# Spreading the last element's rounds by what a tick loads, another PSUM bank for the gate's 1x1, and result rows stored from GpSimd

## The chip, the cores and the metric

The kernel runs on one core of one Trainium2 chip. The metric is the device time of one execution in microseconds (us); lower is better. The core has a matrix engine (TensorE, "PE" in the profile, with its weight loads shown apart as "PEld"), VectorE ("DVE"), ScalarE ("ACT"), GpSimd ("POOL") and SyncE ("SP"), which here only issues DMAs. Each engine carries out its own instructions strictly in the order in which they were written.

## The reference, cut to what matters

The input x is 8 elements of 8 channels of 512x512, in float32. Two layers are each added to their input:

```python
x = x + L0(group_norm(x))        # a few Fourier modes: "spectral" work
x = x + L1(group_norm(x))
# L1(x), per element:
grid = x
for _ in range(15):              # a coupled map lattice
    mapped = 3.9 * grid * (1 - grid)
    grid = 0.85 * (0.7 * mapped + 0.3 * conv3x3_per_channel(mapped)) + 0.15 * x
cml = clip(grid, 1e-4, 1 - 1e-4)
nca = sigmoid(conv1x1(relu(conv3x3(x, 8 -> 128)), 128 -> 8))
g   = sigmoid(conv1x1(relu(conv3x3(concat[x, cml, nca], 24 -> 8)), 8 -> 8))
return g * cml + (1 - g) * nca
```

## The kernel before, in words

Everything is in float32. There are three kinds of work per element, and one schedule that mixes them.

**Steps.** The 15 map steps run on slabs (class `Slabs`): four slabs for the first four channels (`halves[0]`), then four slabs and one `Tail` slab, which holds the last rows, for the other four. One step of one slab is `convolve` (line 524: 48 matrix products into a pair of PSUM tiles) and `settle` (line 537: VectorE adds, line 543: ScalarE squares), and then `renew` exchanges edge rows between slabs by two to four small DMAs from the GpSimd queue (lines 570 and 571); the tail slab gets its edge row through DRAM by SP (lines 580, 641, 646). Step 13 also has a long GpSimd operation on the slab (line 547). A slab's inputs `dE` and `dO` are loaded by SP (line 495), scaled by GpSimd (line 516) and squared once by ScalarE (line 502). A step of a slab needs the slab's own previous step, four or five steps earlier in the order.

**Rounds.** `Hidden.round` is the wide 3x3 convolution (line 723), four image rows in each round, 128 rounds per element; its two halves are evacuated by ScalarE (line 729) and VectorE (line 731). After every second round `Hidden.point` forms the 1x1 channel sum (line 742) in bank 0 of a PSUM tile. It is copied into the tile `y` (line 749) or added to it (line 751); after every fourth round a sigmoid (line 755) finishes `y`, and `y` (128 x 512, 256 KB) is stored to the DRAM plane `nca` (line 758). There is one buffer for `y`, so line 749 of the next four rounds waits until the store has been read out.

**Gates.** `Gate` makes 12 finished image rows; 43 gates make an element. `load` has six DMAs on SP (lines 778 and 783), `conv` is the gate's 3x3 (line 793) with operations on GpSimd (798) and VectorE (799, 803), `point` is its 1x1 (line 810), a sigmoid (814) and a product on GpSimd (816), `finish` adds on VectorE (821) and stores to the output from SP (828). The gates of an element run one element late, beside the steps of the next one. The gates of the last element have no steps to run beside.

**The order.** It is written out by a planner in Python and kept as it is (`keep_order`). A tick (`turn`, `work`) is: two steps, into the PSUM tile pairs `near` and `far`; then loads (`transfers`); then 0, 1 or 2 rounds, into the same pairs; then, where they are due, the gate's 3x3 (bank 0 of `near[0]`), the channel sum (bank 0 of `near[1]`) and the 1x1 of the gate before (bank 1 of `near[0]`). After a tick of two rounds the pairs change places for the next tick; after a tick of one round `near` and `far` change places only for the rest of that tick. Small things put off with `later(1, ...)`, the store of `y` among them, are issued at the end of the tick.

An element has 67 or 68 ticks. In elements 0 to 6 all 128 rounds lie in them, mostly two to a tick. In the last one `ROUNDS_LAST` = 48 rounds are spread evenly over 67 ticks, so a tick has one or none; the 43 gates of element 6 run in the same ticks as early as they can, up to two loaded ahead (`limit` 2). Around the change of phase, from `AHEAD` = 12 steps before the end of the first half to 6 after it, `Phase.fetch` loads the five slabs of the second half; this is called the load window below (ticks 24 to 33 of the element). Only three tile slots are then left to the gates.

After the last step comes the tail of the program: 46 ticks without steps, which hold the remaining 80 rounds, two to a tick, and the 43 gates of the last element, with `limit` 3; its last gate ticks have no round.

Of the kernel before, what the change touches and what calls it, by code (L numbers as in the profile page):

```python
# [43 lines left out]
N = 512  # L44
# [6 lines left out]
FLOOR = -1.0e14  # L51
RT = 32
GR = 12
ROUNDS, ROUNDS_LAST, FIRST_ROUNDS = 128, 48, 8
LONG, LATER, NEXT = -1, -2, -3
GATES_FROM, SPECTRAL_FROM = 1, 2

# [8 lines left out]
SLOTS, SHARED, MORE, LEAST = 20, 5, 8, 3  # L66
AHEAD, PAUSE = 12, 6
# [44 lines left out]
def view(t, offset, dims):  # L112

    return bass.AP(tensor=t.tensor, offset=t.offset + offset, ap=[list(d) for d in dims])
# [3 lines left out]
def conv_layers(ctx: ExitStack, tc: tile.TileContext, a, out):  # L118
    nc = tc.nc
# [9 lines left out]
    class Slots:  # L129
# [4 lines left out]
        def __init__(self, most):  # L134
            self.most, self.held = most, {}
# [15 lines left out]
    sets, shared = Slots(SLOTS), Slots(SHARED)  # L151
# [7 lines left out]
    pairs = [pp.tile([P, 2, N], F32, name=f"pair{i}") for i in range(4)]  # L159
# [4 lines left out]
    def later(ticks, work):  # L164
        put_off.append((now[0] + ticks, work))

    def tick(end=False):
        now[0] += 1
        due = [w for at, w in put_off if end or at <= now[0]]
        put_off[:] = [] if end else [(at, w) for at, w in put_off if at > now[0]]  # L170
        for work in due:
            work()
# [483 lines left out]
    class Phase:  # L656
# [23 lines left out]
        def squares(self, n):  # L680
            while self.squared < len(self.sets) and sets.room():
                if not self.ready(self.squared, 0, n + 2):
                    break
                self.sets[self.squared].square()
                self.squared += 1
# [9 lines left out]
    class Hidden:  # L695
# [42 lines left out]
        def point(self, ps):  # L738

            for r, h in self.hs:  # L740
                for g in range(4):
                    nc.tensor.matmul(  # L742
                        ps[32 * g : 32 * g + 32], w_u[:, r % 4], h[:, g],
                        start=(r == self.hs[0][0]), stop=(r == self.hs[-1][0]),
                        tile_position=(0, 32 * g),
                    )
            if self.hs[0][0] % 4 == 0:
                self.y = wk.tile([P, N], F32, tag="y", name="y", bufs=1)
                nc.scalar.copy(self.y, ps)  # L749
            else:  # L750
                nc.vector.tensor_tensor(self.y, self.y, ps, ALU.add)  # L751
            self.hs.clear()
            if r % 4 == 3:
                y, r0 = self.y, 4 * (r - 3)
                nc.scalar.activation(y, y, AF.Sigmoid, bias=b_u)  # L755

                def store():
                    nc.sync.dma_start(
                        out=view(self.e.nca, (1 + r0) * C * N, [[N, P], [1, N]]), in_=y
                    )  # L760
                    self.e.rows = r0 + 16

                later(1, store)
# [129 lines left out]
    class Others:  # L893


        def __init__(self):
            self.before, self.after, self.limit = None, None, 2
            self.mapped, self.paused = deque(), False
            self.loaded, self.convolved, self.pointed = deque(), deque(), deque()
            self.longs = 0  # L900

        def feed(self, t):
            if self.mapped and not (self.before and self.busy()):
                self.before = self.mapped.popleft()
            e, after = self.before, self.after
            spectral = after and after.pieces
            spectral = spectral and (t >= SPECTRAL_FROM or not e)
            kept = max(0, after.most() - len(after.x)) if spectral else 0
            while e and e.gates and t >= GATES_FROM and not self.paused:
                if len(self.loaded) == self.limit or shared.room() - kept < 2:  # L910
                    break
                if e.rows < min(e.gates[0].r0 + GR + 1, N) or len(e.mapped) <= 2 * SETS:
                    break
                g = e.gates.popleft()
                g.load()
                self.loaded.append(g)
            if spectral:
                after.fetch()
# [62 lines left out]
    def element(b):  # L981
        e = Element(b)
        phase(e.halves[0])
        phase(e.halves[1] + [e.tail])
        elements.append(e)
        return e

    e = element(0)
# [3 lines left out]
    others = Others()  # L992
    for n in count():
# [8 lines left out]
        first = phases[0]  # L1002
# [10 lines left out]
    def work(steps, rounds, e, after, transfers, squares=lambda: None):  # L1013

        settled = iter(())
        near, far = pairs[:2], pairs[2:]
        for (s, step), ps in zip(steps, (near, far)):
            s.convolve(step, ps)
            next(settled, None)
            settled = s.settle(step, ps)  # L1020
            next(settled)
            others.finish()
        others.finish()
        transfers()
        for ps in (near, far)[:rounds]:
            e.hidden.round(ps, after, settled)
        next(settled, None)
        squares()

        if rounds == 2:  # L1030
            pairs.reverse()
        elif rounds:
            near, far = far, near
        point = rounds and e.hidden.n % 2 == 0
        gate = others.gate(near[0][:, 0])
        others.spectral((far[0], far[1]) if gate else (near[0], far[0] if point else near[1]))
        if point:
            e.hidden.point(near[1][:, 0])
        if not others.point(near[0][:, 1]):
            others.spectral([near[0] if gate or point else near[1]])  # L1040
        tick()
        squares()

    def turn(at, rounds, e, after, t):


        now_phases = [p for p in phases if at < p.end + 2]

        def transfers():
            others.feed(t)  # L1050
            for p in now_phases:
                p.fetch(at)

        def squares():
            for p in now_phases:
                p.squares(at)

        for p in now_phases:
            p.prepare(at)
        steps = [slots[i] for i in (at, at + 1) if 0 <= i < len(slots)]  # L1060
        work(steps, rounds, e, after and after.hidden, transfers, squares)
# [3 lines left out]
    at = 0  # L1065
    for b in range(B):
        e = elements[b]
        after = element(b + 1) if b + 1 < B else None
        others.after = after
        done, rounds = e.hidden.n, ROUNDS if after else ROUNDS_LAST  # L1070
        first, second = phases[2 * b : 2 * b + 2]
        ticks = (second.end - at + 1) // 2
        for t in range(ticks):
            assert not after or t < ticks - 5 or not after.pieces
            others.paused = ticks - t <= PAUSE
            if others.paused or first.end - AHEAD <= at < first.end + 6:
                shared.most = LEAST
            else:
                shared.most = MORE if first.at + 6 <= at < first.end else SHARED
            sets.most = SLOTS - shared.most  # L1080
            more = done + (t + 1) * (rounds - done) // ticks - e.hidden.n
            turn(at, min(more, 2 - e.hidden.n % 2), e, after, t)
            at += 2
        assert e.hidden.n == rounds
        assert not others.mapped
        others.mapped.append(e)


    others.after, others.limit, others.paused, shared.most = None, 3, False, SLOTS
    while e.hidden.n < ROUNDS or others.mapped or others.busy():  # L1090
        turn(at, min(2, ROUNDS - e.hidden.n), e, None, GATES_FROM)
        at += 2
    tick(end=True)
    keep_order(tc)
# [54 lines left out]
```

## Time and profile before

| | |
|---|---|
| three runs | 9471.27, 9478.95 and 9484.94 us; median 9478.95 |
| profiled execution | 9485.99 us, of which the span is 9484.2 us |
| busy: PE, DVE, ACT, POOL | 9052.0, 5647.2, 4078.4, 3362.1 us |
| steps on PE (line 524) | 3696.7 us |
| rounds on PE (line 723) | 2854.9 us |
| channel sums, gate 3x3, gate 1x1 on PE (lines 742, 793, 810) | 1062.7, 963.8, 370.3 us |
| store of `y` from SP (line 758) | 256 of them, 256 KB each |
| DMA traffic | 1327 MB, mean 140 GB/s |

A row of a timeline reads: start in us, duration in us, engine and source line, operation, output<-inputs, count; in brackets the time that the engine had been idle before it, and what ended the wait. A row of stretches reads: the stretch, its length, the busy time of each engine with the number of instructions, the clock granted to PE as a share of full speed, the busy share of the DMA engines, GB/s. A row of waits reads: who waited for whom, us in total, how often, the longest.

### The profile page before, as it was taken

What the parts mean: (1) busy time and instruction counts of PE and PEld (TensorE: products, weight loads), DVE (VectorE), ACT (ScalarE), POOL (GpSimd) and SP (SyncE); (2) the same over time, 40 slices, a digit from 0 to 9 for tenths busy, and PEclk for the clock granted to TensorE, in tenths of its full rate; (3) what the DMA queues carried; (4) which work ended last, traced back from release to release, by engine and by line L of the source; (5) the groups of instructions that cost most, each with busy time, mean ns of one, the idle gap of its engine ahead of it and who ended that gap; (6) DMA issues with size and microseconds to landing.
All of it is one profiled execution on the core that took longest, in us unless ns stands there. A gap on an engine that the chain in (4) does not pass through costs nothing. (4 is left out here: it accounts for less than half of the span.)

```text
span 9484.2 us, 331791 instructions
## 1 busy us (share of the span) xinstructions
PE 9052.0 (95%) x148976; PEld 4062.8 (43%) x148976; DVE 5647.2 (60%) x5820; ACT 4078.4 (43%) x4285; POOL 3362.1 (35%) x4422
## 2 busy tenths in 40 slices
PE   6999999999999999999999999999999999988998
PEld 3444444444444444444444444444444444333433
DVE  5665566655665556655566555665566655545555
ACT  2444444444444444444444444444444444434432
POOL 3232334334333343433434343243433433444322
PEclk9999999999999999999999999999999999999999
DMA  4241365555655655655655556565575665675287
GB/s 151 83 128 37 95 170 138 144 138 141 154 151 140 142 132 147 166 132 133 158 134 161 144 118 169 126 162 141 117 181 134 162 138 125 144 164 132 65 207 192
DMA packets 698558, 1327.07 MB, mean 140 GB/s; under 512 B 146938, under 2 KB 152442, under 8 KB 669650
## 3 DMA queue, kind: packets, MB, share of 16 engines
q1 hardware_dynamic: 594432, 1249.10, 52.1%
q0 software_dynamic: 100352, 55.61, 2.9%
q8 instruction: 1171, 19.19, 0.9%
q14 instruction: 249, 2.04, 0.1%
q10 hardware_dynamic: 2354, 1.14, 0.0%
HBM read 977.48 MB, written 270.61 MB: 132 GB/s over the span
## 5 line engine op out<-in xcount | busy, mean ns | idle before, releaser
L524 PE MATMUL pair<-m,band 32*32 32x512 f32 x103680 | 3696.7, 603 | 164.2 <-issue 105.7
L543 ACT ACTIVATE m<-m 128x1024 f32<-128x1024 f32 x2016 | 2128.5, 1056 | 2425.9 <-DVE m L537 2358.8
L723 PE MATMUL pair<-cols,w_p 32*128 32x511 f32 (+1 forms) x24576 | 2854.9, 603 | 59.8 <-DVE m L537 16.4
L524 PEld LDWEIGHTS pair<-m,band 32*32 32x32 f32 x103680 | 1999.4, 103 | 1793.0 <-issue 1006.5
L570 POOL DMA_DIRECT2D m<-m x1568 | 864.1, 551 | 3929.1 <-ACT m L543 3853.4
L537 DVE SCALAR_TENSOR_TENSOR m<-pair,dO 128x1024 f32<-128x1024 f32 x1152 | 1356.6, 1220 | 1187.3 <-PE pair L524 1023.6
L723 PEld LDWEIGHTS pair<-cols,w_p 32*128 32x128 f32 x24576 | 1302.0, 186 | 1627.7 <-issue 1147.9
L537 DVE SCALAR_TENSOR_TENSOR m<-pair,dE 128x1024 f32<-128x1024 f32 x1008 | 1187.8, 1220 | 1106.6 <-PE pair L524 912.8
L731 DVE TENSOR_SCALAR h<-pair,b_p 128x1024 f32<-128x1024 f32 x1024 | 1313.3, 1283 | 870.2 <-PE pair L723 865.3
L729 ACT ACTIVATE h<-pair,b_p 128x1024 f32<-128x1024 f32 x1024 | 1141.4, 1115 | 894.4 <-PE pair L723 893.7
L742 PE MATMUL pair<-h,w_u 128*32 128x512 f32 x8192 | 1062.7, 611 | 42.4 <-ACT h L729 40.8
L793 PE MATMUL pair<-gin,w_g 128*32 128x511 f32 (+1 forms) x8256 | 963.8, 600 | 3.7 <-DMA gin<-nca 2.9
L816 POOL TENSOR_TENSOR mix<-mix 96x512 f32<-96x512 f32 x344 | 438.3, 1274 | 1336.2 <-ACT mix L814 1267.7
L571 POOL DMA_DIRECT2D m<-m x1568 | 844.9, 539 | 30.0 <-issue 25.9
L742 PEld LDWEIGHTS pair<-h,w_u 128*32 128x32 f32 x8192 | 245.2, 110 | 699.8 <-issue 347.3
L755 ACT ACTIVATE y<-y,b_u 128x512 f32<-128x512 f32 x256 | 185.1, 723 | 821.8 <-DVE y L751 821.8
L793 PEld LDWEIGHTS pair<-gin,w_g 128*32 128x32 f32 x8256 | 234.8, 110 | 683.0 <-issue 458.1
L798 POOL TENSOR_TENSOR mix<-mix 96x512 f32<-96x512 f32 x344 | 443.8, 1290 | 73.2 <-DMA mix<-nca 69.1
L547 POOL TENSOR_SCALAR dO<-dO 128x2048 f32<-128x2048 f32 x72 | 391.9, 5443 | 112.4 <-DVE m L537 111.4
L749 ACT COPY y<-pair 128x512 f32<-128x512 f32 x256 | 150.2, 587 | 637.8 <-PE pair L742 510.2
L516 POOL TENSOR_SCALAR dO<-dO,base 128x512 f32<-128x512 f32 x288 | 207.1, 730 | 580.8 <-DMA dO<-xn 502.6
L810 PE MATMUL pair<-mix,w_g 128*32 128x512 f32 x2064 | 370.3, 605 | 42.7 <-DVE mix L803 39.6
(89 smaller groups left out, 3280.9 us busy)
## 6 DMA issues: line engine op xcount, KB each, us to landing
gin<-xn SPq DMA_DIRECT2D x344, 384.0 KB
cols<-xn SPq DMA_DIRECT2D x256, 512.0 KB
x<-in_x SPq DMA_DIRECT2D x120, 1024.0 KB
gin<-cml SPq DMA_DIRECT2D x344, 320.0 KB
gin<-nca SPq DMA_DIRECT2D x344, 320.0 KB
dE<-xn SPq DMA_DIRECT2D x288, 256.0 KB
dO<-xn SPq DMA_DIRECT2D x288, 256.0 KB
mix<-xn SPq DMA_DIRECT2D x344, 192.0 KB
```

Source lines behind the costliest of these rows:

```text
L524: nc.tensor.matmul(ps[h // 2][32 * t : 32 * t + 32, h % 2], band[at, self.channel(step - 1, h, t), dx], m[at, t, dx : dx + N], start=(n == ...
L537: nc.vector.scalar_tensor_tensor(u[:, at], ps[q], FLOOR, d[:, at], ALU.max, ALU.add)
L543: nc.scalar.square(u[:, at], u[:, at])
L570: nc.gpsimd.dma_start(out=view(tb, rb, dims), in_=view(ta, ra, dims))
L571: nc.gpsimd.dma_start(out=view(ta, ra + s, dims), in_=view(tb, rb + s, dims))
L723: nc.tensor.matmul(ps[g // 2][:, g % 2, lo:hi], w_p[p, dx, i % 2], self.cols[p, i // 2, at : at + hi - lo], start=(n == 0), stop=(n == 2), ...
L729: nc.scalar.activation(h[:, :2], ps[0], AF.Relu, bias=b_p)
L731: nc.vector.tensor_scalar(h[:, 2:], ps[1], b_p, 0.0, ALU.add, ALU.max)
L742: nc.tensor.matmul(ps[32 * g : 32 * g + 32], w_u[:, r % 4], h[:, g], start=(r == self.hs[0][0]), stop=(r == self.hs[-1][0]), tile_position ...
L793: nc.tensor.matmul(ps[32 * j : 32 * j + 32, lo:hi], gband[:, dx], gin[:, j, at : at + hi - lo], start=(n == 0), stop=(n == 2), tile_positi ...
L798: nc.gpsimd.tensor_tensor(d, d, ng, ALU.subtract)
L816: nc.gpsimd.tensor_tensor(d, d, mix[: GR * C, 2], ALU.mult)
```

## The change

Five things are changed. The store of `y` is issued by GpSimd instead of SP. The gate's 1x1 goes to bank 1 of `near[1]` where the tick has no channel sum, and stays in `near[0]` where it has one. The pairs also change places after a tick without a round but with a gate's 3x3, and, in the last element alone, after a tick of one round and nothing else. The last element gets 56 rounds instead of 48 in its ticks: two in each tick of the load window, the others spread over the rest; and no gate is loaded in every fifth tick (`closed`). In the tail the other 72 rounds are spread over 39 ticks rather than put two to a tick from the start, and up to four gates are loaded ahead instead of three.

By the written order this gives, in the last element's ticks, 12 more rounds and 6 more channel sums in the load window (19 and 10 instead of 7 and 4, with 5 gate convolutions in both), and 4 rounds and 2 channel sums fewer outside it (37 and 18 instead of 41 and 20, with 38 gate convolutions in both). The tail has 46 ticks as before: 33 full ones (two rounds, channel sum, gate), four with one round and a gate, and five with a gate alone, where it had 38 full ones and four with a gate alone. In elements 1 to 6 two gate 1x1s each change their bank.

```diff
-ROUNDS, ROUNDS_LAST, FIRST_ROUNDS = 128, 48, 8
+ROUNDS, ROUNDS_LAST, FIRST_ROUNDS = 128, 56, 8
...
                 def store():
-                    nc.sync.dma_start(
+                    nc.gpsimd.dma_start(
                         out=view(self.e.nca, (1 + r0) * C * N, [[N, P], [1, N]]), in_=y
                     )
...
-            while e and e.gates and t >= GATES_FROM and not self.paused:
+            while e and e.gates and t >= GATES_FROM and not (self.paused or self.closed):
...
-        if not others.point(near[0][:, 1]):
+        last = others.point((near[0] if point else near[1])[:, 1])
+        if not last:
             others.spectral([near[0] if gate or point else near[1]])
+        if rounds == 0 and gate or rounds == 1 and not (gate or point or last or after):
+            pairs.reverse()
...
+        quota = [(t + 1) * (rounds - done) // ticks for t in range(ticks)]
+        if not after:
+            loads = [first.end - AHEAD <= at + 2 * t < first.end + 6 for t in range(ticks)]
+            left = rounds - done - 2 * sum(loads)
+            quota = [
+                2 * sum(loads[: t + 1]) + (t + 1 - sum(loads[: t + 1])) * left // (ticks - sum(loads))
+                for t in range(ticks)
+            ]
...
-            more = done + (t + 1) * (rounds - done) // ticks - e.hidden.n
+            more = done + quota[t] - e.hidden.n
+            others.closed = not after and t % 5 == 4
...
-    others.after, others.limit, others.paused, shared.most = None, 3, False, SLOTS
-    while e.hidden.n < ROUNDS or others.mapped or others.busy():
-        turn(at, min(2, ROUNDS - e.hidden.n), e, None, GATES_FROM)
+    others.after, others.limit, others.paused, others.closed = None, 4, False, False
+    shared.most = SLOTS
+    done, ticks = e.hidden.n, -(-N // GR) - 4
+    for t in count():
+        if e.hidden.n == ROUNDS and not others.mapped and not others.busy():
+            break
+        more = min(ROUNDS, done + (t + 1) * (ROUNDS - done) // ticks) - e.hidden.n
+        turn(at, min(more, 2 - e.hidden.n % 2), e, None, GATES_FROM)
         at += 2
```

More of the change, by code (lines that the diff above doesn't have):

```diff
@@ L897, in __init__ @@
             self.before, self.after, self.limit = None, None, 2
-            self.mapped, self.paused = deque(), False
+            self.mapped, self.paused, self.closed = deque(), False, False
             self.loaded, self.convolved, self.pointed = deque(), deque(), deque()
```

## The prediction

> **What bounds the kernel now.** I read the page first, then stretches, then who PE waited for in the last element, then the timeline where it waits longest.
>
> ```profile
> PE 9052.0 (95%) x148976; PEld 4062.8 (43%) x148976; DVE 5647.2 (60%) x5820; ACT 4078.4 (43%) x4285; POOL 3362.1 (35%) x4422
> PE   6999999999999999999999999999999999988998
> ```
>
> PE is the bound: nine tenths or more in nearly every slice. The exceptions are the first slice, which the change leaves alone, and the last seven. So time can only come from work taken off PE, and the change takes none off, or from PE's idle time, which is 432 us in all. The stretches say where that lies (last element's ticks: 8073 to 8998, its load window 8412 to 8586; then the tail).
>
> ```profile
> 0.00:8073.00 8073.00, 7780.64 (x129534) 3545.01 (x129537) 4915.12 (x5125) 3569.16 (x3747) 2858.98 (x3820) 0.99 0.55 138
> 8073.00:8412.00 339.00, 311.79 (x5814) 131.54 (x5798) 181.32 (x181) 137.91 (x142) 150.10 (x211) 0.98 0.63 145
> 8412.00:8586.00 174.00, 135.85 (x2356) 54.41 (x2340) 76.71 (x70) 56.79 (x59) 87.78 (x102) 0.89 0.71 164
> 8586.00:8998.00 412.00, 376.17 (x7488) 173.71 (x7460) 228.75 (x216) 171.38 (x173) 156.98 (x205) 0.99 0.39 93
> 8998.00:9060.00 62.00, 47.39 (x372) 18.07 (x367) 18.36 (x19) 13.39 (x16) 7.33 (x6) 0.83 0.71 179
> 9060.00:9437.00 377.00, 377.00 (x3340) 134.83 (x3335) 212.30 (x196) 125.06 (x142) 87.79 (x71) 1.00 0.86 209
> 9437.00:9484.20 47.20, 23.20 (x152) 5.18 (x144) 14.64 (x16) 4.72 (x7) 13.15 (x10) 0.79 0.51 126
> ```
>
> In the last element's 925 us PE is idle for 27.2 + 38.2 + 35.8 = 101 us, and in the load window its clock also falls to 0.89. In the tail it is idle 14.6 us at the start and 24.0 us at the end, and never in the 377 us between. What it waited for from 8073 to 8998:
>
> ```profile
> PE pair L810 <- DVE mix L803: 27.1, 25, 4.5
> PE pair L742 <- ACT h L729: 17.6, 10, 6.8
> PE pair L524 <- ACT mix L814: 13.6, 13, 3.1
> PE pair L524 <- ACT h L729: 9.0, 8, 1.3
> ```
>
> The first, third and fourth are small waits in almost every tick, one of each kind here:
>
> ```profile
> 8815.19 1.06 PE L810 MATMUL pair<-mix,w_g 128*32 128x512 f32 x6 [1.08 <-DVE mix L803]
> 8817.17 5.40 PE L524 MATMUL pair<-m,band 32*32 32x512 f32 x156 [0.92 <-ACT mix L814]
> ...
> 8840.42 6.17 PE L524 MATMUL pair<-m,band 32*32 32x512 f32 x173 [1.26 <-ACT h L729]
> ```
>
> The 1x1 waits until VectorE has read the gate's 3x3 out of the same tile. The next step waits until ScalarE has read the 1x1, or the only round, out of the pair that the step wants. In full ticks of two rounds the same pieces lie far enough apart. The second wait, 17.6 us, is the load window: ScalarE stands at a slab's square until `dE` has landed (43.8 us in this element), and a round's evacuation queues behind it. At the start of the tail it is SP:
>
> ```profile
> 9002.98 7.31 SPq L758 DMA_DIRECT2D nca<-y  x1
> 9019.18 0.59 ACT L749 COPY y<-pair 128x512 f32<-128x512 f32 x1 [15.04 <-DMA nca<-y]
> 9019.82 5.09 PE L723 MATMUL pair<-cols,w_p 32*128 32x512 f32 x24 [11.56 <-ACT y L749]
> ```
>
> The store of `y` stood 7.31 us in SP's issue behind 21 stores of `cml` (its median is 0.34 us), the one `y` buffer stayed taken, and PE stood for 11.56 us.
>
> **Part 1, the bank and the exchange of pairs.** Nothing is added on PE. Outside the load window the last element has 11 ticks without a round but with gate and 1x1 (each loses about 1.08 + 0.92 = 2.0 us), 13 of one round, gate and 1x1 (0.87 us each, one row of that wait) and 6 of one round alone (1.26 us). All have other PE work of one tick in between afterwards: 22.0 + 11.3 + 7.6 = 41 us. After the change five ticks have a 1x1 and neither round nor gate; there the pairs do not change and the step waits 0.9 us for the sigmoid: 4.5 us back. Net 36 us. The work just after a wait also runs slower: a tick of one round, sum, gate and 1x1 holds 15.6 us of PE work after such a tick against 14.6 us elsewhere. With some seven of these I take 8 us. In elements 1 to 6 a 0.87 us wait goes once each, and the other exchanged 1x1 already waited for nothing: 5 us.
>
> **Part 2, rounds into the load window.** Its ten ticks gain 12 rounds of 2.85 us and 6 sums of 2.0 us, 46 us of PE work. What ten ticks with two rounds cost under the same loads is seen one element earlier. The first row is element 6's window, 20 rounds and 10 sums; the second is the last element's, 7 rounds and 4 sums:
>
> ```profile
> 7341.00:7504.70 163.70, 158.24 (x2673) 75.80 (x2671) 115.73 (x118) 79.98 (x82) 79.18 (x88) 0.99 0.66 178
> 8412.50:8585.70 173.20, 135.05 (x2326) 53.82 (x2321) 76.41 (x70) 56.79 (x59) 87.28 (x102) 0.89 0.71 163
> ```
>
> So the time there is set by the loads, and work put into it is nearly free. PE work after: ten pairs of steps at 6.28 us (a tick with nothing else), 19 rounds, 10 sums, five gates at 2.78 + 1.06 us: 62.8 + 54.2 + 20 + 19.2 = 156 us. With idle time between element 6's 5.5 us and element 5's 12 us, and a little for the clock, 167 us: 6 us less than now. Outside the window 4 rounds and 2 sums go and one 1x1 comes: 14 us less.
>
> **Part 3, the tail.** Its gates now come every 10.63 us (36 of them), then 7.38, 7.31, 7.24 and 9.08 us where there is no round; the first two distances are 9.78 and 16.97. Sum from first to last: 440.5 us. After: 33 at 10.63 (350.8), two at 7.8 (less one round), two that PE could do in 5.8 but that I hold at the 7.3 us of the ticks without rounds, which wait for loads, and five without rounds at 6.4 (between PE's 3.9 and 7.3, since a gate more is loaded ahead): 413 us. Add 4 us for a wait at the start, which stays. The first gate comes 30 us after 8998 now. Its loads are queued behind the same `cml` stores, so it comes at 28 us even with the store of `y` elsewhere; the two single-round ticks leave less work to cover it, and that work is done later in the count above. 16 us follow the last gate in both. Tail: 461 instead of 486 us, 25 less. DMA moves about 92 MB there; at 209 GB/s and a 0.86 share the engines' full rate is estimated at 243 GB/s, hence a floor of 380 us.
>
> **Part 4, the store from GpSimd.** 256 issues leave SP, where SP stood 868 us for the sigmoid over elements 0 to 6; but behind the store SP next meets line 828, which waits 2244 us for line 821, so little is freed. The nearest row for an issue on GpSimd is line 570: 552 ns median for 24 KB or 8 KB, 32 packets each. This store has at least 128 rows, so 0.55 to 4 x 0.55 = 2.2 us; I take 1.1. It is placed at the end of a tick, ahead of the next edge exchange on GpSimd, which idles there for 7.76 us before line 570 at 8815. If that cover is gone, as at step 13 where operations of 5.4 us follow one another, 16 such places cost up to 16 x 2.2 = 35 us. From below: the 124.9 us that squares wait for `dE` might fall by a tenth, -12 us. I take -3, since most ticks lie near the idle row.
>
> The Trainium skill, "DMA: Bandwidth & Descriptors", section "Issuing engines are not separate DMA queues", speaks against this part: whichever engine issues, the transfers share the same DMA engines, so only issue time is saved. The 7.31 us above is issue time, but the landing at 9019 came later than that. By the rule the two waits of 11.56 and 2.79 us at the tail's start stay, and the sum would be some 10 us less gain; no sum here needs it.
>
> **Sum.** Window -6, outside it -36 - 8 - 14 = -58, tail -25, elements 1 to 6 -5, store -3: -97 us. Against the profiled execution, 9485.99 us, that is 9389; its median of three is 7 us lower, so 9382, rounded to 9385 us.
>
> **Rivals.** *Only part comes* (0.20): more rounds in the window bring more evacuations behind a late `dE`, the 38 us idle stays there and the tail's DMAs do not get ahead. Window 156 + 38 = 194 instead of 167 (+27), tail's single-round and last ticks at 10.6 (+20): 9432, or 9420 to 9450. For it: loads cannot be seen to come earlier. Against: element 6's window. *More comes* (0.08): SP, free of the store, gets edge rows and slabs in earlier in all elements, and half of their 30 us idle each goes for two or three: 9345. *No change* (0.05): PE's waits reappear at the next hand-over of a bank, 9460 to 9498. *Slower* (0.07): the store holds GpSimd before the edge exchange in every element. At 1.1 us each, all exposed, 256 x 1.1 = 282: 9667. It decides from 95 / 256 = 0.37 us exposed per store. Against it: GpSimd is busy 35%, and the next exchange must await a step and its squares first.
>
> **How the numbers follow.** The forecast, 9385, has 0.60 (9350 to 9420). The range leaves out the slower case, no change, the upper edge of the partial one and some of the larger gain: 9342 to 9448. About 0.2%, 19 us, can be told from no change: faster 0.88 (0.60 + 0.20 + 0.08), same 0.05, slower 0.07.
>
> **What would show it.** Right: in the last element waits of 1x1 for line 803 and of steps for line 814 nearly gone; ten window ticks of about 167 us with two rounds each; line 749 not waiting for its store at the tail's start; gates of the tail still 10.63 us apart in full ticks. Wrong: GpSimd's line 758 at over 2 us with line 570 late behind it, the window at 190 us or more, or a longer wait for the first gate's loads than 30 us.

## The result and the profile after

The changed kernel takes 9507.52 us (median of 17 runs, 9477.40 to 9526.49), the kernel before 9482.33 us (17 runs, 9463.76 to 9503.76). The ratio is 1.0026, 95% interval 1.0015 to 1.0036: slower by about 25 us, where 97 us less were forecast. The profiled execution of the changed kernel took 9518.56 us with a span of 9516.7, against 9485.99 and 9484.2 before, so the two traces differ by 32.5 us.

The page of the changed kernel, its busy line and TensorE's line of slices:

```profile
PE 9080.2 (95%) x148976; PEld 4064.1 (43%) x148976; DVE 5655.6 (59%) x5820; ACT 4072.7 (43%) x4285; POOL 3505.6 (37%) x4678
PE   6999999999999999999999999999999999999989
```

Of the three slices below nine tenths among the last five one is left, and the kernel is still slower. PE ran as many matrix products as before, in 28 us more. The stretches of the changed kernel, cut at the same places of the program (elements 0 to 6; the last element before, in and after its load window; start, middle and end of the tail):

```profile
0.00:8149.00 8149.00, 7817.80 (x129534) 3543.38 (x129536) 4904.18 (x5125) 3565.02 (x3747) 2976.90 (x4040) 0.99 0.54 137
8149.00:8462.00 313.00, 293.14 (x5643) 125.99 (x5634) 169.99 (x167) 132.19 (x135) 144.28 (x210) 0.96 0.55 129
8462.00:8649.00 187.00, 169.99 (x2695) 73.43 (x2678) 100.81 (x85) 73.44 (x76) 90.83 (x106) 0.94 0.68 160
8649.00:9049.00 400.00, 378.43 (x7432) 172.88 (x7431) 229.24 (x219) 170.03 (x174) 172.87 (x219) 0.97 0.48 113
9049.00:9110.00 61.00, 37.34 (x372) 13.87 (x352) 21.12 (x19) 9.91 (x11) 6.70 (x6) 0.80 0.74 175
9110.00:9470.00 360.00, 360.00 (x3182) 128.10 (x3178) 211.79 (x190) 116.71 (x135) 96.30 (x86) 1.00 0.88 219
9470.00:9516.70 46.70, 23.49 (x185) 6.45 (x174) 18.44 (x19) 5.39 (x8) 17.75 (x13) 0.86 0.59 142
```

The first row has it: the last element, in whose ticks and tail nearly all of the change but the store lies, starts 76 us later. There the same 129,534 products were 37 us longer busy (7780.6 before) and PE stood some 39 us longer. The last element and the tail gained 43.5 us. By ticks, each taken from the start of VectorE's first addition of a step to the next tick's (a profiled execution is one run, and runs of one kernel lie up to 50 us apart, so what a part is worth is taken from medians below):

| us, profiled executions | before | after | difference | forecast |
|---|---|---|---|---|
| elements 0 to 6 | 8073.5 | 8149.5 | +76.0 | -8 |
| last element, load window | 173.1 | 187.0 | +13.9 | -6 |
| last element, other ticks | 741.6 | 712.5 | -29.1 | -58 |
| tail | 496.0 | 467.7 | -28.3 | -25 |

In the last element the prediction's list of waits before the change leaves out two rows that stand above its last one:

```profile
PE pair L524 <- issue: 17.5, 12, 3.1
PE pair L524 <- DMA m<-m: 9.8, 4, 4.0
```

The waits of the changed kernel there (who waited for whom, us in total, times, longest):

```profile
PE pair L524 <- DMA m<-m: 17.1, 7, 3.8
PE pair L524 <- issue: 11.1, 7, 3.6
PE pair L524 <- ACT mix L814: 10.7, 5, 2.2
PE pair L742 <- ACT h L729: 6.8, 7, 5.3
```

Of the 27.1 us for line 803 2.0 are left, and of the 9.0 us of steps for line 729 0.8. Line 814 is down to the five ticks with a 1x1 and neither round nor 3x3, at 2.1 us each instead of the 0.9 that I took. At the top are now steps that wait for the edge exchange (`m<-m`), 17.1 us where it was 9.8, and steps whose wait shows no cause in the profile ("issue"). At the start of the tail:

```profile
9064.38 8.32 SPq L778 DMA_DIRECT2D gin<-xn  x1
...
9087.05 4.53 PE L793 MATMUL pair<-gin,w_g 128*32 128x512 f32 x24 [23.28 <-DMA gin<-nca]
```

The store of `y` no longer stands behind the stores of `cml`; the gate's first load stands there in its place for 8.32 us, and PE waits 23.28 us for the gate.

### The profile page after: what moved, and what is told of

Same layout as the page of the kernel before. It is cut to its first block, busy times and chain, and to the rows that moved or that the text cites. A ratio compares the mean times of both kernels' runs of the same rounds, so it can differ in the third digit from the quotient of the medians.

```text
span 9516.7 us, 331665 instructions
## 1 busy us (share of the span) xinstructions
PE 9080.2 (95%) x148976; PEld 4064.1 (43%) x148976; DVE 5655.6 (59%) x5820; ACT 4072.7 (43%) x4285; POOL 3505.6 (37%) x4678
## 5 line engine op out<-in xcount | busy, mean ns | idle before, releaser
L723 PE MATMUL pair<-cols,w_p 32*128 32x511 f32 (+1 forms) x24576 | 2867.6, 605 | 44.6 <-DVE m L537 20.9
L821 DVE SCALAR_TENSOR_TENSOR mix<-mix,back 96x512 f32<-96x512 f32 x344 | 334.9, 974 | 143.9 <-POOL mix L816 143.9
L803 DVE TENSOR_SCALAR mix<-pair,b_g 128x512 f32<-128x512 f32 x344 | 257.7, 749 | 201.5 <-PE pair L793 200.3
```

Of the source, the lines that this page charges most:

```text
L723: nc.tensor.matmul(ps[g // 2][:, g % 2, lo:hi], w_p[p, dx, i % 2], self.cols[p, i // 2, at : at + hi - lo], start=(n == 0), stop=(n == 2), ...
```

## The experiments

Each of the twelve was timed beside the kernel before on the same chip, in three batches on three chips (first to fourth, fifth to eighth, ninth to twelfth), so runs of different batches are compared by their ratios. "First" to "twelfth" below follows the order of the runs.

### Which part costs: first and second

The first is the kernel before with only the store of `y` moved; the second is all of the change but that.

```diff
 # first, on the kernel before
-                    nc.sync.dma_start(
+                    nc.gpsimd.dma_start(
 # second, on the changed kernel
-                    nc.gpsimd.dma_start(
+                    nc.sync.dma_start(
```

> The kernel before, with the store of y issued by GpSimd and nothing else of the change. In the changed kernel's profiled execution the last element began 76.0 us later than before (8149.5 against 8073.5 us), and everything from there on was 43.5 us shorter. Theory A, the store does it by its place in GpSimd's order (it stands for the sigmoid, and slab scaling and edge exchange stand behind it): elements 0 to 6 longer by 50 to 75 us here too, 9530 to 9555 us. Theory B, the store does it by its path (256 KB through GpSimd's DMA queue, shared with the edge exchange): the same number. Theory C, SP is let go earlier and its loads collide with the edge exchange: the same number. Theory D, it is not the store: no change within 10 us of 9482.

> The changed kernel, with the store of y issued by SP as before. Theories A, B and C: elements 0 to 6 as before, the last element and the tail keep most of their gain of 43.5 us: 9435 to 9450 us. At the tail's start the wait for the store of y may come back, which takes some 5 us of it. Theory D: like the changed kernel, about 9507.

Measured: the store alone 9545.71 us, ratio 1.0068 (1.0052 to 1.0085); the rest alone 9442.81 us, ratio 0.996 (0.9947 to 0.9974). The product is 1.0028, within the interval of the change's own 1.0026. So one word of the diff costs some 66 us (against 9479.15 there), and the other parts gain some 36.

### What of the store costs: third, fourth, fifth, tenth, twelfth

Four theories stood: the store's place in GpSimd's order (A); its path through GpSimd's queue (B); SP, let go by it, issues its own loads too early (C); something other than the store (D, gone with the first run).

The third puts the store, in elements 0 to 6, behind the next tick's first edge exchange on GpSimd; the fourth issues it from ScalarE, which computes the sigmoid and need not wait for it.

```diff
 # third
-                later(1, store)
+                if self.e.b < B - 1:
+                    pending.append(store)   # issued behind the next tick's first exchange
+                else:
+                    later(1, store)
 # fourth
-                    nc.sync.dma_start(
+                    nc.scalar.dma_start(
```

> The kernel before, with the store of y issued by GpSimd, but in elements 0 to 6 placed one half tick later: after the next tick's first edge exchange, when the sigmoid is long done. Theory A (place): GpSimd no longer stands for the sigmoid, and the time is back at 9475 to 9495 us. Theories B (path) and C (SP let go): still 9530 to 9555.

> The kernel before, with the store of y issued by ScalarE, which makes y itself and so never stands for it. SP is let go as with GpSimd, and GpSimd's queue is left alone. Theories A and B: 9470 to 9490 us, as before or a little less. Theory C: 9530 to 9555.

Measured: later in the order 9534.90 us, 1.0061 (1.0045 to 1.0078); from ScalarE 9524.69 us, 1.0045 (1.0030 to 1.0060). The place hardly matters, so A falls. Most of the loss comes without GpSimd too.

The fifth and the twelfth leave the store on GpSimd and on ScalarE and give SP back only its wait: a copy of 64 bytes of `y`, issued where the store was. The tenth is the mirror: the store stays on SP, and GpSimd gets the small copy and so the wait.

```diff
 # fifth (store on GpSimd) and twelfth (store on ScalarE)
+                    nc.sync.dma_start(out=scratch, in_=y[0:1, 0:16])
                     self.e.rows = r0 + 16
 # tenth (store on SP)
+                    nc.gpsimd.dma_start(out=scratch, in_=y[0:1, 0:16])
                     self.e.rows = r0 + 16
```

> The kernel before with the store of y from GpSimd, as in the first experiment (9546 us, ratio 1.0068), and one more DMA: where SP issued the store it now copies 64 bytes of y into a DRAM scratch that nobody reads. SP so waits for the sigmoid at the old place, while the 256 KB still leave through GpSimd. Theory C (with SP let go, slabs and gates are loaded earlier and collide with the small edge-exchange DMAs): back to 9475 to 9500, ratio 0.9995 to 1.002; the stretch from 0 to the start of element 7 again about 8075 to 8085 us instead of 8134. Theory B (what counts is the path, that is GpSimd's own time for issuing the store and its bulk before the exchange on the same queue): stays at 9530 to 9550, ratio 1.0055 to 1.0075. A value between splits the loss between the two.

> The kernel before, store of y on SP as ever, and one DMA more: at the store's place GpSimd copies 64 bytes of y into a DRAM scratch that nobody reads. It is the mirror of the fifth experiment: GpSimd now stands for the sigmoid where the store from GpSimd stood, but nothing is let go on SP and no 256 KB go through its queue. The fifth still lost 21 us (ratio 1.0022). If that rest is GpSimd's standing ahead of the edge exchange, ratio 1.0015 to 1.003, 9500 to 9515. If it is the 256 KB taken out of the way of SP's loads, no change: 0.9993 to 1.0007.

> The fourth experiment (store of y from ScalarE; 9525 us, ratio 1.0045) with the 64-byte copy of y by SP at the old place, as in the fifth. If letting SP go is the whole loss of the ScalarE store: 0.9995 to 1.0008. If what remained in the fifth (1.0022) is the 256 KB no longer standing ahead of SP's loads in the same queue, which holds for any other engine, the same 1.0015 to 1.003 here. With the store from ScalarE GpSimd never stands for the sigmoid, so a rest here is not GpSimd's.

Measured, with the runs without the copy:

| store from | SP let go | SP waits as before |
|---|---|---|
| SP | | 1 (the kernel before) |
| SP, GpSimd waits too | | 1.0005 (0.9996 to 1.0015), 9489.61 us |
| ScalarE | 1.0045 (1.0030 to 1.0060), 9524.69 us | 0.9998 (0.9987 to 1.0008), 9487.17 us |
| GpSimd | 1.0068 (1.0052 to 1.0085), 9545.71 us | 1.0022 (1.0011 to 1.0033), 9506.59 us |

Down the columns GpSimd costs 0.0023 and 0.0024 over ScalarE; along the rows letting SP go costs 0.0047 and 0.0046. The two add. SP's freedom is two thirds of the loss, some 44 us, and a 64-byte DMA takes it back. The rest, some 22 us, belongs to the path through GpSimd; its wait for the sigmoid alone, 0.0005, is not told from nothing, so what is left is the issue or the transfer of the store in that queue, which no run has by itself. Nor does a run hold back the gates' loads alone, so which of SP's freed transfers do the harm is read from one place of the traces.

What SP waited for, over the whole execution: first the kernel before, then the store alone on GpSimd, then the same with the 64-byte copy (which is line 761 there, and moves line 828 to 829).

```profile
SPq L828 <- DVE mix L821: 2787.5, 333, 26.5
SPq L580 <- ACT m L543: 1055.5, 137, 28.4
SPq L758 <- ACT y L755: 973.4, 211, 7.8
```

```profile
SPq L828 <- DVE mix L821: 3539.0, 333, 28.8
SPq L580 <- ACT m L543: 1349.5, 135, 31.7
```

```profile
SPq L829 <- DVE mix L822: 2804.0, 332, 27.7
SPq L580 <- ACT m L543: 1056.7, 135, 26.8
SPq L761 <- ACT y L755: 975.2, 212, 8.5
```

The 973 us at line 758 moved to line 828 (+752) and line 580 (+294). In sum SP is no freer, but what stands between line 758 and those lines is issued earlier. Here is that in one tick of element 6. The timeline of the first experiment (store alone on GpSimd), with GpSimd's and SP's DMAs:

```profile
7002.01 0.56 POOL L570 DMA_DIRECT2D m<-m  x1 [7.97 <-ACT m L543]
...
7002.78 0.34 SPq L778 DMA_DIRECT2D gin<-xn  x1
...
7004.97 0.42 SPq L783 DMA_DIRECT2D mix<-nca  x1
...
7008.43 0.60 POOL L758 DMA_DIRECT2D nca<-y  x1 [2.86 <-ACT y L755]
...
7017.67 7.39 PE L723 MATMUL pair<-cols,w_p 32*128 32x511 f32 x36 [2.65 <-issue]
```

And of the fifth, where SP waits:

```profile
6986.58 0.56 POOL L570 DMA_DIRECT2D m<-m  x1 [10.57 <-ACT m L543]
...
6992.73 0.23 SPq L761 DMA_DIRECT2D scratch<-y  x1
6993.00 0.60 POOL L758 DMA_DIRECT2D nca<-y  x1 [2.86 <-ACT y L755]
6993.14 0.33 SPq L779 DMA_DIRECT2D gin<-xn  x1
```

Without the wait the six loads of a gate go out between the exchange's own DMAs; with it they go out 5 us behind them. The exchange issued from 7002.01 landed 5.9 to 8.4 us after its issues, the one from 6986.58 after 2.6 to 3.9 us. The stretches around the stall in the first experiment:

```profile
7003.00:7009.00 6.00, 6.00 (x118) 2.28 (x125) 4.38 (x4) 1.07 (x2) 3.12 (x5) 1.00 0.99 210
7009.00:7015.00 6.00, 6.00 (x139) 3.02 (x110) 4.19 (x4) 2.69 (x3) 1.30 (x4) 1.00 1.07 212
7015.00:7017.60 2.60, 0.02 (x2) 0.00 (x0) 0.52 (x1) 0.48 (x1) 0.93 (x2) 0.81 0.89 322
7017.60:7025.00 7.40, 7.33 (x38) 3.00 (x38) 1.28 (x1) 2.71 (x3) 2.74 (x5) 0.61 0.18 55
```

The DMA engines are full for about 15 us in a row (the last column but one; in the fifth it is 11 us, from 6994 to 7005, and PE does not stand), PE then stands for 2.6 us, and the next 7.4 us run at a granted clock of 0.61. The tick took 24.9 us; the same tick took 18.3 us in the fifth and before. A stall of 2.65 us cost 6.6. Against the fifth, this tick loses 6.1 to 6.6 us in three of the seven elements. It is the worst tick; the one ahead of it took 2.6 us longer in the fifth in this element (23.5 against 20.9 us).

The stall is one for which the profile shows no wait ("issue"), but the trace of DMA packets tells what ended it. One DMA queue of the page is of the kind "instruction" (packets, MB, share of the engines):

```profile
q8 instruction: 1171, 19.19, 0.9%
```

That is a packet of 16 KB for every 254 of the 297,952 records of PE and its weight loads, in all versions alike, so it can be read as the queue that brings PE its instructions. Here such a packet landed 1.30 us before PE went on. In the first experiment, from 300 us on, PE has 51 waits over 1 us that end on "issue", and each of them ends 1.2 to 1.75 us after such a packet landed; of the 68 other waits over 1 us four do, about what chance gives. In the kernel before it is 46 of 47 against none of 58. The late packets come when the DMA engines are full: in the first experiment, from 979 to 8060 us, 34 of 40 follow 8 us with the engines over 0.9 busy, and 210 of the 856 others. So PE stood there for its own instructions, as far as these traces can tell, and not for data.

What stays open is how much of the loss goes this way. From 979 to 8060 us (the end of element 0 and elements 1 to 6; the slower a run, the less of the program lies in it, at most 1%) the line of steps says what PE's idle time before them ended on (after count, busy us and mean ns: idle us, then its parts); before, then the store on GpSimd, GpSimd with SP's wait, ScalarE, ScalarE with SP's wait:

```profile
L524 PE MATMUL pair<-m,band 32*32 32x512 f32 x80093 | 2837.3, 601 | 98.8 <-issue 83.3 <-ACT h L729 8.7 <-DMA m<-m 3.7
```

```profile
L524 PE MATMUL pair<-m,band 32*32 32x512 f32 x79488 | 2827.5, 602 | 120.3 <-issue 93.6 <-DMA m<-m 14.3 <-ACT h L729 8.6
```

```profile
L524 PE MATMUL pair<-m,band 32*32 32x512 f32 x79778 | 2833.1, 602 | 96.9 <-issue 71.5 <-DMA m<-m 11.7 <-ACT h L729 8.6
```

```profile
L524 PE MATMUL pair<-m,band 32*32 32x512 f32 x79872 | 2835.7, 600 | 104.9 <-issue 84.5 <-DMA m<-m 9.2 <-ACT h L729 8.4
```

```profile
L524 PE MATMUL pair<-m,band 32*32 32x512 f32 x80064 | 2844.0, 603 | 88.8 <-issue 70.2 <-ACT h L729 8.4 <-DVE y L751 4.3
```

With SP's wait there are 16 to 23 us less idle time than without, most of it "issue"; waits for the exchange (`m<-m`) are few where the store is not on GpSimd and SP waits. The kernel before has more "issue" time (83.3 us) than both runs with SP's wait, so single profiles do not give the size to better than some 12 us. The mean landing of the exchange's DMAs of line 570 in that time is the same in all of them (5.38 to 5.42 us): the harm lies in few ticks. How it is shared between late exchanges and late instructions stays open.

### What the other parts are worth: sixth, seventh, eleventh

All but the eleventh start from the second experiment (0.996).

```diff
 # sixth: no other bank, no added exchange of pairs
-        last = others.point((near[0] if point else near[1])[:, 1])
+        last = others.point(near[0][:, 1])
-        if rounds == 0 and gate or rounds == 1 and not (gate or point or last or after):
-            pairs.reverse()
 # seventh: no closed ticks
-            others.closed = not after and t % 5 == 4
 # eleventh: the kernel before, with closed ticks
+            others.closed = not after and t % 5 == 4
```

> The second experiment (all of the change but the store; 9443 us, ratio 0.996) without the other bank of the gate's 1x1 and without the added exchanges of pairs. By the prediction's terms this gives back 36 + 8 us in the last element and 5 us in elements 1 to 6: 9485 to 9495, ratio 1.0007 to 1.0017. If most of the gain came from the tail alone, 9445 to 9460, ratio 0.9965 to 0.998. In the last element the 1x1's waits for the addition (27 us before) should be back.

> The second experiment (9443 us, ratio 0.996) without the rule that no gate is loaded in every fifth tick of the last element: by the written order each tick then loads one gate, none loads two. If two gates loaded at once delay the edge exchange (steps that waited 2.6 to 3.0 us for it after such ticks), some 10 ticks win 1 to 2 us each: 9425 to 9435, ratio 0.994 to 0.9955, and the waits of line 524 for the exchange in the last element fall. If closing was worth having, 9450 to 9465, ratio 0.9965 to 0.9985.

> The kernel before with one thing of the change: no gate is loaded in every fifth tick of the last element. If the price found by leaving it out of the change (about 32 us) is its own, by doubled loads, ticks that lose their overlap and 1x1s that stand alone: 9505 to 9520, ratio 1.0025 to 1.004. If it hurts only beside the other parts, 9485 to 9495, ratio 1.000 to 1.001. If it helps here, as the first waits of the load window might suggest, under 9480.

Measured: without the bank and the exchange of pairs 9498.56 us, 1.0016 (1.0005 to 1.0027), so bank and exchange are worth 0.0056, some 53 us. Without the closed ticks 9410.83 us, 0.992 (0.9906 to 0.9933): closing them cost 0.0040, some 38 us. On the kernel before, closing alone costs 1.0017 (1.0005 to 1.0030), some 16 us, between the two cases that were expected.

In the last element without bank and exchange the old waits are back:

```profile
PE pair L524 <- ACT mix L814: 23.6, 14, 3.1
PE pair L810 <- DVE mix L803: 20.5, 20, 2.5
```

The ticks outside the load window take 754.6 us there against 707.7 in the second, and 675.9 without the closed ticks. The last stretch of the last element, of the second and then the seventh experiment:

```profile
8566.00:8960.00 394.00, 373.54 (x7452) 171.61 (x7444) 231.15 (x219) 170.12 (x174) 169.90 (x214) 0.98 0.49 116
```

```profile
8574.00:8931.00 357.00, 350.73 (x7290) 166.62 (x7284) 218.99 (x206) 167.27 (x169) 157.02 (x205) 1.00 0.44 103
```

PE idles 20 us in the one and 6 in the other, and the clock is at 1.00 rather than 0.98. The expectation looked for the gain in the waits for the exchange; those stay (18.6 and 17.3 us in the last element). What goes is another thing. A closed tick loads no gate, so the next one loads two, has a 1x1 without a 3x3, and the one after it a 3x3 without a 1x1. Outside the load window the second experiment has 9 ticks of the first kind right after a closed one, which idle 11.7 us, and 10 of the second, which idle 11.4 us; in the seventh there are one and two such ticks, with 0.3 us. A stall of that kind is also followed by slower work. The timeline of the second experiment, a 1x1 alone and the step behind it:

```profile
8127.32 1.06 PE L810 MATMUL pair<-mix,w_g 128*32 128x512 f32 x6
8128.31 1.05 PE L524 MATMUL pair<-m,band 32*32 32x512 f32 x4
8131.46 8.04 PE L524 MATMUL pair<-m,band 32*32 32x512 f32 x188 [2.11 <-ACT mix L814]
```

A whole step of 192 products takes 6.58 us in the ticks before; here 188 take 8.04, after a stall of 2.11.

### A kernel better than both: eighth and ninth

The eighth is the second with the store of `y` on GpSimd only where no exchange and no steps follow, from the last round of the last element's ticks on, and with the tail's rounds rounded up, so that its first ticks are full. The ninth also leaves out the closed ticks.

```diff
-        more = min(ROUNDS, done + (t + 1) * (ROUNDS - done) // ticks) - e.hidden.n
+        more = min(ROUNDS, done - (-(t + 1) * (ROUNDS - done) // ticks)) - e.hidden.n
-                    nc.sync.dma_start(
+                    (nc.gpsimd if self.e.b == B - 1 and r >= ROUNDS_LAST - 1 else nc.sync).dma_start(
 # ninth, besides
-            others.closed = not after and t % 5 == 4
```

> The second experiment (9443 us, ratio 0.996) with the store of y from GpSimd only from the last round of the last element's ticks on, where no edge exchange follows, and with the tail's rounds rounded up, so that its first ticks are full. The store's wait at the tail's start (a tick of 20.8 us, 7 us of it PE idle, against 10.6 for a full tick) should go, since SP has nothing of y left to issue: 5 to 10 us less, 9430 to 9440, ratio 0.9945 to 0.996. If instead the gate's own loads take the store's place behind the stores of cml, as in the changed kernel (8.3 us in SP's issue), it is the same as the second experiment, 9438 to 9448.

> The seventh and eighth experiments together: all of the change but the closed ticks, y stored by SP up to the last round of the last element's ticks and by GpSimd from there on, the tail's rounds rounded up. Leaving out the closed ticks took the last element's ticks outside the load window from 707.7 to 675.9 us; the eighth took the tail from 475.6 to 453.9. Different places, so they should add: 9443 - 32 - 22 to 25 = 9386 to 9389, by the two ratios (0.992 x 0.9924 / 0.996 = 0.9884) 9372 to 9380 at the 9482 to 9490 of the kernel before. I say 9375 to 9392. If both only let the same stall go, 9405 to 9412, ratio 0.992.

Measured: the eighth 9409.52 us, 0.9924 (0.9908 to 0.9940), better than expected; of its gain over the second, 22 us lie in the tail (475.6 to 453.9), and some 12 are not placed. The changed kernel, whose tail takes 467.7 us, differs there from the second only by the store, so about 8 of the 22 us are the store and 14 the rounding up. The ninth takes 9392.39 us, 0.9903 (0.9887 to 0.9920), just past the upper end of what was expected; the ratio by adding, 0.9884, lies just outside the interval, so the gains add for the most part. It beats the kernel before by about 93 us. Its page and its tail's start:

```profile
PE   6999999999999999999999999999999999999999
```

```profile
8964.02 8.21 SPq L778 DMA_DIRECT2D gin<-xn  x1
...
8986.91 4.76 PE L793 MATMUL pair<-gin,w_g 128*32 128x512 f32 x24 [14.25 <-DMA gin<-nca]
```

SP still stands 8.21 us behind the stores of `cml`, as in the changed kernel, and the first gate comes 37 us after the tail's start, as in the second experiment; but PE idles 14.25 us rather than 22.6, as it has two rounds more to do meanwhile. So the gain at this place is the rounding up, not the store. The store's gain comes later: between the third and the fourth gate lie 20.8 us in the second experiment, with PE waiting 7.34 us for line 749 and so for the store of `y`, and 10.63 us in the changed kernel, the eighth and the ninth.

## Why the prediction was wrong

**The step that failed is Part 4**, the store from GpSimd, at -3 us with bounds of -12 and +35. "Behind the store SP next meets line 828, which waits 2244 us for line 821, so little is freed" is right in its sum: the 973 us reappear there and at line 580. It is wrong in what it leaves out: six loads of a gate stand between the store and line 828 in SP's order, and in the tick shown SP's wait for the sigmoid was what kept them off the edge exchange and the DMA engines from being full for 15 us in a row. The bounds took only the price of the issue on GpSimd; a wait that goes was held to be harmless at worst. It measured 1.0068, some 66 us, over the upper bound, 0.0046 of it from SP's freedom (shown by the 64-byte copies) and the rest from GpSimd's queue; that the gates' loads are what does the harm is argued from the tick. The Trainium skill, "DMA: Bandwidth & Descriptors", section "Issuing engines are not separate DMA queues", says that issuing from another engine only saves issue time, since the transfers share the DMA engines. That they share them agrees with the full DMA engines above; that the choice saves or costs no more does not: with the same traffic the time moved by 0.0045, because other loads went out at other times.

**A part was not priced at all**: the closed ticks stand in the change and have no term in the sum. They cost 16 us on the kernel before and some 38 in the changed order. Of the 122 us between forecast and result the store is 69, the closed ticks 38 and the load window 20 (by the two profiles); the other parts came out somewhat better than forecast.

**Part 1 was right in size.** 36 + 8 + 5 = 49 us were forecast, 0.0056 or 53 us measured. Only the place was off: the 5 us of elements 1 to 6 do not show, and 14 us of it lie in the tail (475.6 against 489.2 us), whose ticks with a gate and few rounds also use the other bank and exchange the pairs. With Part 2's 14 us outside the window the forecast there was -58; without the closed ticks it is 741.6 - 675.9 = 66 us, with them 34 (second experiment) or 29 (changed kernel).

**Part 2, the window, was mis-sized**: 167 us forecast, 187.0 measured, where 173.1 was before. PE's work took 170 us rather than 156 (clock 0.94) and the idle time was 17 rather than 11. Element 6's window, on which it leaned, was the shortest of its kind: 163.7 us, where those of elements 1 to 5, also with 20 rounds, took 168.4 to 174.1 in the same profile, element 5's the longest. It also holds one gate and not five. The bytes do not tell them apart (29.1 MB there, 29.9 in the changed kernel's window), so why the window takes 187 us and not 174 stays open; of its idle time 6.0 us are channel sums waiting for a late evacuation (line 729), 3.3 us steps waiting for the exchange and 3.1 us "issue".

**Part 3 was right in size**, 28.3 us against 25, not in its reasons: full ticks are 10.63 us as forecast, but the first gate comes 42.6 us after the tail's first tick instead of 39.6, by line 803, and two thirds of what the second experiment gains there go with the bank (13.6 of 20.4 us).

**Rivals.** "Slower" was the case, by another mechanism than the one written down: not GpSimd standing before the exchange (0.0005 where measured). Its deciding point, 0.37 us per store, was worked out against a gain of 95 us; the gain was 36. "Only part comes", 9420 to 9450 with a window of 194, fits the change with its store left on SP by its numbers, 9443 and 187, but the time partly by luck: the other half of its loss was put into the tail, which came out as forecast, while the closed ticks, which it does not name, cost 38 us.

**Readings.** Two readings of the profile before were too broad. Not all of the last seven slices lie below nine tenths, but three of the last five. The small waits were not in almost every tick: the three rows count 25, 13 and 8 waits in 67 ticks, and the two rows left out, 27.3 us together, are the kinds of wait that the store's move made longer in elements 0 to 6.

## What to carry to other kernels

A wait ahead of one DMA also holds back every DMA that its engine issues after it. Before a store is moved off a queue, list what stands between it and that queue's next wait, and ask what those transfers will meet when they go out earlier; a 64-byte DMA that keeps the old wait tests this at almost no cost. Price every line of a change, the small rule about every fifth tick as well: here it took about half of what the other parts gained, 38 of some 75 us. Where TensorE stands without a cause in the profile, look whether its instructions came late behind full DMA engines.

## What the runs showed of the hardware that was not expected

Short stalls of TensorE cost more than their length: after 2.65 us the granted clock was 0.61 for the next 7.4 us and the tick lost 6.6 us; after 2.11 us it was 0.65 for 4.5 us, and a step of 6.58 us took more than 8. In elements 0 to 6 the changed kernel has 39 us more idle time and 37 us more busy time for the same products. The Trainium skill, "TensorE: Matmul & The Clock Gate", section "What's actually happening", says that the clock falls to one half after an idle window of about 3.4 us; here gaps of 2.11 and 2.65 us were enough, and in the latter the clock fell to 0.50 when PE had stood for 1.6 us. Both gaps follow thin work: 4 products in 1.05 us and 12 in 1.99 us.

TensorE's waits over 1 us that end on "issue" end 1.2 to 1.75 us after a packet of the instruction queue has landed (51 of 51 in the first experiment, 46 of 47 before), and 34 of 40 such late packets follow 8 us of DMA engines over 0.9 busy.

On GpSimd the 256 KB store took about 0.6 us to issue, about half of what I had taken (1.1 us), and ScalarE could issue it at no measurable cost (0.9998) once SP kept its wait.
